# Loads of X^T, W and the Toeplitz tile issued at other places of a channel's order, each large load behind a compute instruction

## The chip, the cores and the metric

The kernel runs on one core of a Trainium2 chip. The metric is the device time of one execution in microseconds. Beside three timed executions there is one that the hardware profiler recorded; durations, waits and distances below come from that one. It has its own device time (878.34 us), and a span, from the program's first instruction to its last (876.5 us).

## The reference

For each of 64 channels (C) and a batch of 4, on images of 256 x 256 in float32:

```
k[c]  = outer product of two learned filters hx[:, c], hy[:, c]
y     = causal 2-D convolution of x with k       (written as an FFT of size 512)
x1    = y + x * bias[c]
scores = x1 @ x1^T / sqrt(256)                    (per image)
red   = sum over t of scores[s, t] * weights[c, s, t]
y2    = x1 + red
out   = (y2 - mean) * rsqrt(var + 1e-5) * gamma[c] + beta[c]
        (mean and var over batch, rows and columns of the channel)
```

Because the 2-D kernel is an outer product, the convolution is two 1-D convolutions, one along each axis. Each is a multiplication by a Toeplitz matrix.

## The kernel before

The 64 channels are worked one after the other, each in three groups of TensorE work, written by hand in an order that the kernel keeps (`manual_schedule`); the framework only adds the semaphores that the data needs, and allots buffers.

- `conv_z(c, m)`, m = 0, 1 (line 209): multiplies X^T by the Toeplitz rows along one axis, into PSUM. `copy_z` (218, ScalarE) copies each half out to the tile z.
- `conv_x0(c)` (234): multiplies z by the Toeplitz rows along the other axis. `add_bias` (244, VectorE) adds x * bias and writes x1.
- `gram(c, v)`, v = 0, 1 (297): x1 @ x1^T, in blocks. On VectorE `weigh` follows (317 and 321: product with W, pr and two partial sums) and `spread` (331). After both halves `all_sum` (339, GpSimd) sums over the partitions and gives red.

The rest of a channel comes later, in the iterations of the next channels. In iteration c, with p = c-1, q = c-2, f = c-3, e = c-4: `pick_red(p)` (346, ScalarE) waits for the sum over the partitions and copies half of red; `add_red(p)` (353, VectorE) adds red and sums; `minus_mean(q)` (388, 389) and `squares(q)` (393) are ScalarE's; `root(q)` (405 to 409) too; `finish` (433) scales a quarter of channel f or e on ScalarE, and its output transfer (434) is issued right behind it from SP.

All large transfers of the loop are issued by SP in one queue, in the order of the program. Per channel these are four outputs (256 KB each), four quarters of X^T by `load_xt` (256 KB each), W by `load_w` (320 KB), and the Toeplitz tile in four quarters by `load_h(c+2, 0..3)` (36 KB each, line 186). An output waits for ScalarE's finish. The Toeplitz tile has only its lower 64 partitions loaded; `copy_h` (191, ScalarE), the first ScalarE instruction of an iteration, copies them to the upper 64, and `conv_z` reads both halves: its second matmul reads the upper one. The tile of channel c+2, loaded in iteration c, is copied at the start of iteration c+1, and read by conv_z(c+2) in that iteration.

TensorE's order in iteration c is conv_x0(c), conv_z(c+1, 0), conv_z(c+1, 1), gram(c, 0), gram(c, 1). The loop runs to c = 61; `last_channels` has the rest in an order of its own, which the diff leaves as it is.

Of the kernel before, what the change touches and what calls it, by code (L numbers as in the profile page):

```python
# [9 lines left out]
AF = mybir.ActivationFunctionType  # L10
# [5 lines left out]
B, C, S = 4, 64, 256  # L16
# [21 lines left out]
def conv_scores_bn_kernel(  # L38
# [19 lines left out]
    nc = tc.nc  # L58
# [6 lines left out]

    xts, ws, hs = {}, {}, {}

    def load_xt(c, v, n):
        if not n:
            xts[c, v] = ld.tile([P, 4, S], F32, tag=f"xt{v}", name=f"xt_{c}_{v}", bufs=4)  # L70
        part = bass.ts(n, 2)
        nc.sync.dma_start(xts[c, v][:, part], xT[c, v, :, part])

    PARTS = ((0, 0), (1, 0), (0, 1), (1, 1))

    def load_w(c):
        w = ld.tile([P, 10, H], F32, tag="w", name=f"w_{c}", bufs=2)
        nc.sync.dma_start(w, wl[c])
        ws[c] = w


# [94 lines left out]
    def load_h(c, n):  # L176


        if not n:
            hs[c] = ld.tile([P, 2, GW], F32, tag="toep", name=f"toep_{c}")  # L180
        src = bass.AP(
            g_dram.tensor, g_dram.offset + c * 2 * GW + 16 * n,
            [[4 + C * 2 * GW, COPIES], [1, 4], [1, GW + S]],
        )
        rows = hs[c][bass.ts(n, 16)].rearrange("p a r -> p (a r)")
        nc.sync.dma_start(rows[:, : GW + S], src)

    def copy_h(c):

        toep = hs[c]  # L190
        nc.scalar.copy(toep[H:, :, :S], toep[:H, :, :S])  # L191
# [5 lines left out]
    st8, zs = {}, {}  # L197

    def conv_z(c, m):


        toep = hs[c]
        p1 = [ps.tile([P, 2, S], F32, tag="ps", name=f"p1_{c}_{m}_{u}") for u in range(2)]
        for k in range(2):
            for i in range(4):
                for t in range(4):
                    u, v = t % 2, t // 2
                    rows = bass.ts(u, H)
                    nc.tensor.matmul(  # L209
                        p1[u][bass.ts(v, H), k, : S - H * i],  # L210
                        lhsT=xts[c, v][rows, i, bass.ts(2 * m + k, H)],
                        rhs=toep[rows, 1, H * i : S], start=(i == 0), stop=(i == 3),
                    )
        return p1

    def copy_z(c, m, p1):
        for u in range(2):
            nc.scalar.copy(zs[c][:, u, bass.ts(m, 2), :], p1[u][:, :, ::-1])  # L218

    def conv_x0(c, z, parts=range(2)):  # L220

# [50 lines left out]
    def begin(c):  # L272
        x0 = wk.tile([P, 2, 4, S], F32, tag="x0", name=f"x0_{c}", bufs=5)
        red0 = sm.tile([P, B, 2], F32, tag="red0", name=f"red0_{c}")
        sp = wk.tile([P, B, S], F32, tag="sp", name=f"sp_{c}")
        pr = wk.tile([P, B, S], F32, tag="pr", name=f"pr_{c}")
        rd = wk.tile([P, B, S], F32, tag="rd", name=f"rd_{c}")
        st8[c] = (x0, red0, sp, pr, rd)
# [3 lines left out]
    def gram(c, v, weighed=True):  # L282


        xb = st8[c][0].rearrange("p v i (t s) -> p v i t s", s=H)
        gs = [ps.tile([P, 8, H], F32, tag="ps", name=f"g_{c}_{v}_{u}") for u in range(2)]

        for places in (
            ((0, slice(0, 3), slice(0, 5, 2)), (1, slice(1, 4), slice(2, 7, 2))),
            ((2, slice(2, 4), slice(3, 7, 3)), (3, slice(0, 4, 3), slice(0, 4, 3))),  # L290
        ):
            for i in range(4):
                for n in range(4):
                    u, h = n % 2, n // 2
                    rows = bass.ts(u, H)
                    m, t, o = places[h]
                    nc.tensor.matmul(  # L297
                        gs[u][bass.ts(h, H), o, :],
                        lhsT=xb[rows, v, i, m, :], rhs=xb[rows, v, i, t, :],
                        start=(i == 0), stop=(i == 3),  # L300
                    )
        if not weighed:
            banks.extend(gs)
            return
        for u in range(2):
            weigh(c, 2 * v + u, gs[u])
        if c < BY_PE:
            for u in range(2):
                spread(c, 2 * v + u)

    def weigh(c, b, g):

        _, red0, _, pr, _ = st8[c]
        w = ws[c]
        for n, part in enumerate((ROW0, ROW1)):
            junk = wk.tile([P, 3, H], F32, tag="junk", name=f"junk_{c}_{b}_{n}")
            nc.vector.scalar_tensor_tensor(  # L317
                junk, g[:, part, :], 1.0 / math.sqrt(S), w[:, 3 * n : 3 * n + 3, :],
                ALU.mult, ALU.mult, accum_out=red0[:, b, n : n + 1],
            )  # L320
        nc.vector.scalar_tensor_tensor(  # L321
            pr[:, b].rearrange("p (t s) -> p t s", s=H), g[:, COL, :], 1.0 / math.sqrt(S),
            w[:, 6:10, :], ALU.mult, ALU.mult,
        )

    def spread(c, b):

        _, red0, sp, pr, _ = st8[c]
        for n in range(2):
            part = bass.ts(n, P)  # L330
            nc.vector.scalar_tensor_tensor(  # L331
                sp[:, b, part], eye_sb, red0[:, b, n : n + 1], pr[:, b, part],
                ALU.mult, ALU.add,
            )
# [13 lines left out]
    def add_red(c):  # L348

        x0, _, _, _, rd = st8[c]  # L350
        mom = sm.tile([P, 8], F32, tag="mom", name=f"mom_{c}")
        for v in range(2):
            nc.vector.scalar_tensor_tensor(  # L353
                x0[:, v], x0[:, v], 1.0, rd[:, 2 * v, None, :].to_broadcast([P, 4, S]),
                ALU.mult, ALU.add, accum_out=mom[:, v : v + 1],
            )
        nc.gpsimd.partition_all_reduce(mom[:, 2:4], mom[:, 0:2], P, RED.add)  # L357
        return mom
# [27 lines left out]

    def minus_mean(mom):
        nc.scalar.activation(mom[:, 4:5], mom[:, 2:3], AF.Identity, bias=mom[:, 3:4])  # L388
        nc.scalar.activation(mom[:, 5:6], mom[:, 4:5], AF.Identity, scale=-1.0 / (B * S * S))

    def squares(c, mom, v):
        sq = wk.tile([P, 4, S], F32, tag="sq", name=f"sq_{c}_{v}", bufs=1)
        nc.scalar.activation(  # L393
            sq, st8[c][0][:, v], AF.Square, bias=mom[:, 5:6], accum_out=mom[:, 6 + v : 7 + v]
        )

    def sum_squares(c, mom):
        tot = sm.tile([P, 3], F32, tag="tot", name=f"tot_{c}")
        nc.gpsimd.partition_all_reduce(tot[:, 0:2], mom[:, 6:8], P, RED.add)  # L399
        return tot  # L400
# [25 lines left out]
    def finish(c, g, sh, v, n, vector=False):  # L426
        part = bass.ts(n, 2)
        o = wk.tile([P, 2, S], F32, tag="o", name=f"o_{c}_{v}_{n}", bufs=8)
        y = st8[c][0][:, v, part]
        if vector:  # L430
            nc.vector.tensor_scalar(o, y, g, sh, ALU.mult, ALU.add)
        else:
            nc.scalar.activation(o, y, AF.Identity, bias=sh, scale=g)  # L433
        nc.sync.dma_start(out[c, v, n], o)
# [130 lines left out]
    def begin_z(c):  # L565
        zs[c] = wk.tile([P, 2, 4, S], F32, tag="z", name=f"z_{c}")
# [6 lines left out]
    for c in range(C - 2):  # L573
        p, q, f, e = c - 1, c - 2, c - 3, c - 4
        begin(c)
        copy_h(c + 1)
        if e >= 0:
            finish(*fins[e], 0, 1)
        if c + 2 < C and c:
            load_xt(c + 2, 1, 1)  # L580
        load_h(c + 2, 0)
        conv_x0(c, zs.pop(c))
        if q >= 0:
            minus_mean(moms[q])
            squares(q, moms[q], 0)
        if e >= 0:
            finish(*fins[e], 1, 0)
        if c + 3 < C:
            load_xt(c + 3, 0, 0)
        load_h(c + 2, 1)  # L590
        if q >= 0:
            squares(q, moms[q], 1)
            tot = sum_squares(q, moms[q])
        if f >= 0:
            fins[f] = (f, *scale_shift(f, moms.pop(f), *scales.pop(f)))
        begin_z(c + 1)
        copy_z(c + 1, 0, conv_z(c + 1, 0))
        if e >= 0:
            finish(*fins.pop(e), 1, 1)
        load_h(c + 2, 2)  # L600
        if c + 3 < C:
            load_xt(c + 3, 1, 0)
        load_w(c + 1)
        load_h(c + 2, 3)
        copy_z(c + 1, 1, conv_z(c + 1, 1))
        if p >= 0:
            pick_red(p)
        if f >= 0:
            finish(*fins[f], 0, 0)
        if c + 3 < C:  # L610
            load_xt(c + 3, 0, 1)
        if q >= 0:
            scales[q] = root(q, tot)
        gram(c, 0)
        if p >= 0:
            moms[p] = add_red(p)
        gram(c, 1)
        if c < BY_PE:
            all_sum(c)
# [72 lines left out]
```

## Time and profile before

| | |
|---|---|
| median of 3 executions | 879.99 us (877.52 to 881.45) |
| profiled execution | 878.34 us, span 876.5 us |
| TensorE matmuls, weight loads | busy 98%, 96% of the span |
| VectorE, ScalarE, GpSimd | busy 86%, 71%, 49% |
| DMA queue of SP | 165.52 MB, 57.5% of 16 engines' time |
| output, X^T, W, Toeplitz transfers | 256, 256, 64 and 252 issues |

In rows of the timeline the first number is the start in us, the second the time taken; then the engine and the line of the kernel, the operation, what is written from what is read, and how many instructions were merged. SPq rows are the issue of a transfer, not its movement: when its data land stands in the records of the packets. In the waits view a row says which engine and line stood, for whom, how many us in total, how many times, and the longest. In square brackets stands the idle time before an instruction and what ended it. The start of a channel's conv_z is that of its first weight load of line 209.

### The profile page before, as it was taken

The numbers are of one execution on the slowest core, as the hardware profiler recorded it, in microseconds if no ns is written. First come the engines' busy times: TensorE is split into PE (matmuls) and PEld (weight loads), VectorE is DVE, ScalarE is ACT, GpSimd is POOL, SyncE is SP. The second block draws the span as 40 slices with busy tenths as digits, with TensorE's granted clock in tenths as the row PEclk, the third lists the DMA queues.
The fourth block names the chain that finished last, engine by engine and source line by source line (L and its number), as shares of the span: only waits on it lengthen the run. The fifth ranks groups of instructions, "written<-read, shape, count | busy, mean of one in ns | idle before, by whom it ended". The sixth has DMA issues, their size and how long they took to land.

```text
span 876.5 us, 55956 instructions
## 1 busy us (share of the span) xinstructions
PE 856.5 (98%) x24676; PEld 841.9 (96%) x24676; DVE 754.8 (86%) x2642; ACT 620.5 (71%) x1212; POOL 425.4 (49%) x195
## 2 busy tenths in 40 slices
PE   7999999999999999999999999999999999999993
PEld 5999999999999999999999999999999999999992
DVE  3588898898898898898898898898898898898886
ACT  2256777777776777777777776776777776776785
POOL 0236546545545545545645645645545545645600
PEclk9999999999999999999999999999999999999998
DMA  6624666666556565666566666666566666566534
GB/s 188 221 76 141 204 196 205 193 206 205 197 200 205 192 203 202 200 204 206 191 208 198 200 203 201 199 206 201 183 208 200 196 204 199 189 203 209 190 141 169
DMA packets 89870, 169.69 MB, mean 194 GB/s; under 512 B 10555, under 2 KB 11740, under 8 KB 89628
## 3 DMA queue, kind: packets, MB, share of 16 engines
q1 hardware_dynamic: 88972, 165.52, 57.5%
q8 instruction: 194, 3.18, 1.6%
q10 hardware_dynamic: 656, 0.59, 0.2%
q14 instruction: 48, 0.39, 0.2%
HBM read 98.18 MB, written 67.76 MB: 189 GB/s over the span
## 4 chain that ended last, share of the span: by engine, by line
PE 97%; DVE 1%; DMA 0%; ACT 0%; issue 0%; ACTq 0%; DVEq 0%
PE g L297 32%; PE p L209 32%; PE p L234 31%; PE p L263 0%; DMA fw_sb<-in_fw 0%; PE rp L368 0%; PE rp L373 0%; PE idle L166 0%; DVE x L382 0%; ACT o L433 0%; PE ph L146 0%; PE ph L130 0%; DVE fa L133 0%; DVE junk L317 0%; DVE fa L138 0%
## 5 line engine op out<-in xcount | busy, mean ns | idle before, releaser
L339 POOL PARTITION_ALL_REDUCE rd<-sp x61 | 373.5, 6124 | 182.3 <-DVE sp L331 182.3
L209 PE MATMUL p<-toep,xt 64*64 64x128 f32 (+3 forms) x8192 | 303.7, 297 | 0.6 <-issue 0.5
L297 PE MATMUL g<-x 64*64 64x192 f32 (+1 forms) x8192 | 302.1, 296 | 0.0
L234 PE MATMUL p<-toep,z 64*64 64x128 f32 (+3 forms) x8064 | 298.9, 296 | 0.0
L209 PEld LDWEIGHTS p<-toep,xt 64*64 64x64 f32 x8192 | 292.3, 133 | 5.7 <-PE idle L166 1.1
L234 PEld LDWEIGHTS p<-toep,z 64*64 64x64 f32 x8064 | 292.3, 133 | 4.1 <-issue 0.4
L297 PEld LDWEIGHTS g<-x 64*64 64x64 f32 x8192 | 288.6, 133 | 0.5 <-issue 0.2
L317 DVE SCALAR_TENSOR_TENSOR junk<-g,w 128x192 f32<-128x192 f32 x512 | 161.0, 352 | 83.0 <-PE g L297 83.0
L433 ACT ACTIVATE o<-x,sh,g 128x512 f32<-128x512 f32 x253 | 204.2, 811 | 3.1
L244 DVE SCALAR_TENSOR_TENSOR x<-xt,chan_sb,p 128x512 f32<-128x512 f32 x256 | 174.0, 741 | 8.4 <-PE p L263 7.3
L218 ACT COPY z<-p 128x512 f32<-128x512 f32 x256 | 134.7, 577 | 27.0 <-PE p L209 27.0
L393 ACT ACTIVATE sq<-x,mom 128x1024 f32<-128x1024 f32 x128 | 146.4, 1144 | 4.4 <-DVE x L382 2.0
L353 DVE SCALAR_TENSOR_TENSOR x<-x,rd 128x1024 f32<-128x1024 f32 x122 | 144.2, 1219 | 0.1
L331 DVE SCALAR_TENSOR_TENSOR sp<-eye_sb,red,pr 128x128 f32<-128x128 f32 x488 | 138.0, 345 | 0.0
L357 POOL PARTITION_ALL_REDUCE mom<-mom x61 | 24.4, 401 | 231.6 <-DVE x L353 227.5
L346 ACT COPY rd<-rd 64x512 f32<-64x512 f32 x61 | 37.6, 616 | 127.9 <-POOL rd L339 127.9
L321 DVE SCALAR_TENSOR_TENSOR pr<-g,w 128x256 f32<-128x256 f32 x256 | 107.4, 420 | 0.0
L191 ACT COPY toep<-toep 64x512 f32<-64x512 f32 x63 | 38.9, 618 | 42.8 <-DMA toep<-g_dram 32.6
L317 DVE DVE_READ_ACCUMULATOR junk<-g,w 128x1 f32 x512 | 42.5, 83 | 0.0
L388 ACT ACTIVATE mom<-mom 128x1 f32<-128x1 f32 x62 | 18.1, 292 | 32.0 <-POOL mom L357 31.8
L399 POOL PARTITION_ALL_REDUCE tot<-mom x62 | 29.8, 481 | 9.4 <-ACT sq L393 9.4
L393 ACT ACTIVATION_READ_ACCUMULATOR sq<-x,mom 128x1 f32 x128 | 23.8, 186 | 0.0
(62 smaller groups left out, 217.1 us busy)
## 6 DMA issues: line engine op xcount, KB each, us to landing
xt<-in_xT SPq DMA_DIRECT2D x256, 256.0 KB
out<-o SPq DMA_DIRECT2D x256, 256.0 KB
w<-in_wl SPq DMA_DIRECT2D x64, 320.0 KB
toep<-g_dram SPq DMA_DIRECT2D x252, 36.0 KB
g_dram<-g_sb SPq DMA_DIRECT2D x1, 320.0 KB
g_dram<-g_sb ACTq DMA_DIRECT2D x1, 320.0 KB
decay_sb<-in_decay SPq DMA_DIRECT2D x1, 256.0 KB
fw_sb<-in_fw ACTq DMA_DIRECT2D x1, 192.0 KB
```

Source lines behind the costliest of these rows:

```text
L209: nc.tensor.matmul(p1[u][bass.ts(v, H), k, : S - H * i], lhsT=xts[c, v][rows, i, bass.ts(2 * m + k, H)], rhs=toep[rows, 1, H * i : S], sta ...
L218: nc.scalar.copy(zs[c][:, u, bass.ts(m, 2), :], p1[u][:, :, ::-1])
L234: nc.tensor.matmul(p2[v][bass.ts(u, H), i, : S - H * k], lhsT=z[rows, u, k, bass.ts(2 * m + i, H)], rhs=toep[rows, 0, H * k : S], start=(k ...
L244: nc.vector.scalar_tensor_tensor(st8[c][0][:, v, part], xts[c, v][:, part], chan_sb[:, 0, c : c + 1], p2[v][:, :, ::-1], ALU.mult, ALU.add,)
L297: nc.tensor.matmul(gs[u][bass.ts(h, H), o, :], lhsT=xb[rows, v, i, m, :], rhs=xb[rows, v, i, t, :], start=(i == 0), stop=(i == 3),)
L317: nc.vector.scalar_tensor_tensor(junk, g[:, part, :], 1.0 / math.sqrt(S), w[:, 3 * n : 3 * n + 3, :], ALU.mult, ALU.mult, accum_out=red0[: ...
L321: nc.vector.scalar_tensor_tensor(pr[:, b].rearrange("p (t s) -> p t s", s=H), g[:, COL, :], 1.0 / math.sqrt(S), w[:, 6:10, :], ALU.mult, A ...
L331: nc.vector.scalar_tensor_tensor(sp[:, b, part], eye_sb, red0[:, b, n : n + 1], pr[:, b, part], ALU.mult, ALU.add,)
L339: nc.gpsimd.partition_all_reduce(rd.rearrange("p b s -> p (b s)"), sp.rearrange("p b s -> p (b s)"), P, RED.add)
L353: nc.vector.scalar_tensor_tensor(x0[:, v], x0[:, v], 1.0, rd[:, 2 * v, None, :].to_broadcast([P, 4, S]), ALU.mult, ALU.add, accum_out=mom[ ...
L393: nc.scalar.activation(sq, st8[c][0][:, v], AF.Square, bias=mom[:, 5:6], accum_out=mom[:, 6 + v : 7 + v])
L433: nc.scalar.activation(o, y, AF.Identity, bias=sh, scale=g)
```

## The change

Five transfers per channel get an extra semaphore wait on SP: a load is issued only after a certain instruction of ScalarE or VectorE has ended (`behind`, which adds a dependency on a marked instruction). The places in SP's order change with it. Before and after, for one iteration c of the loop:

```
before                         after
out finish(e,0,1)              out finish(e,0,1)
xt (c+2,1,1)                   toep(c+2) quarter 0
toep(c+2) quarter 0            xt (c+2,1,1)     after the mean of q (389)
out finish(e,1,0)              out finish(e,1,0)
xt (c+3,0,0)                   toep(c+2) quarter 1
toep(c+2) quarter 1            xt (c+3,0,0)     after copy_z(c+1, 0), u = 0
out finish(e,1,1)              out finish(e,1,1)
toep(c+2) quarter 2            toep(c+2) quarter 2
xt (c+3,1,0)                   w (c+1)          after copy_z(c+1, 1), u = 1
w (c+1)                        xt (c+3,1,0)     after pr of b = 0 (321)
toep(c+2) quarter 3            out finish(f,0,0)
out finish(f,0,0)              toep(c+2) quarter 3
xt (c+3,0,1)                   xt (c+3,0,1)     after add_red(p), v = 0 (353)
```

In the program gram(c, 0) now stands ahead of pick_red(p), finish(f, 0, 0) and root(q). The core of the diff:

```diff
+    marks = {}
+
+    def behind(load, place):
+        if place in marks:
+            tc.add_manual_dep(
+                load.ins, marks[place].ins.name,
+                mybir.DependencyInfo(mybir.DependencyClass.Sync, mybir.DependencyReason.DATA),
+                reason="pace of the loads",
+            )
...
-        nc.sync.dma_start(xts[c, v][:, part], xT[c, v, :, part])
+        load = nc.sync.dma_start(xts[c, v][:, part], xT[c, v, :, part])
+        behind(load, place)
...
-        nc.sync.dma_start(w, wl[c])
+        load = nc.sync.dma_start(w, wl[c])
+        behind(load, place)
...
         copy_h(c + 1)
         if e >= 0:
             finish(*fins[e], 0, 1)
-        if c + 2 < C and c:
-            load_xt(c + 2, 1, 1)
         load_h(c + 2, 0)
         conv_x0(c, zs.pop(c))
         if q >= 0:
             minus_mean(moms[q])
             squares(q, moms[q], 0)
+        if c + 2 < C and c:
+            load_xt(c + 2, 1, 1, "mean")
         if e >= 0:
             finish(*fins[e], 1, 0)
-        if c + 3 < C:
-            load_xt(c + 3, 0, 0)
         load_h(c + 2, 1)
...
         copy_z(c + 1, 0, conv_z(c + 1, 0))
+        if c + 3 < C:
+            load_xt(c + 3, 0, 0, ("z", 0, 0))
         if e >= 0:
             finish(*fins.pop(e), 1, 1)
         load_h(c + 2, 2)
+        copy_z(c + 1, 1, conv_z(c + 1, 1))
+        load_w(c + 1, ("z", 1, 1))
+        gram(c, 0)
         if c + 3 < C:
-            load_xt(c + 3, 1, 0)
-        load_w(c + 1)
-        load_h(c + 2, 3)
-        copy_z(c + 1, 1, conv_z(c + 1, 1))
+            load_xt(c + 3, 1, 0, ("pr", 0))
         if p >= 0:
             pick_red(p)
         if f >= 0:
             finish(*fins[f], 0, 0)
-        if c + 3 < C:
-            load_xt(c + 3, 0, 1)
+        load_h(c + 2, 3)
         if q >= 0:
             scales[q] = root(q, tot)
-        gram(c, 0)
         if p >= 0:
             moms[p] = add_red(p)
+        if c + 3 < C:
+            load_xt(c + 3, 0, 1, ("add", 0))
         gram(c, 1)
```

More of the change, by code (lines that the diff above doesn't have):

```diff
@@ L66, in conv_scores_bn_kernel, with load_xt @@
     xts, ws, hs = {}, {}, {}
-    def load_xt(c, v, n):
+    marks = {}
[6 more added lines that the diff above has]
+            )
+    def load_xt(c, v, n, place=None):
         if not n:
@@ L71, in load_xt, with load_w @@
         part = bass.ts(n, 2)
-        nc.sync.dma_start(xts[c, v][:, part], xT[c, v, :, part])
+        load = nc.sync.dma_start(xts[c, v][:, part], xT[c, v, :, part])
+        behind(load, place)
     PARTS = ((0, 0), (1, 0), (0, 1), (1, 1))
-    def load_w(c):
+    def load_w(c, place=None):
         w = ld.tile([P, 10, H], F32, tag="w", name=f"w_{c}", bufs=2)
-        nc.sync.dma_start(w, wl[c])
+        load = nc.sync.dma_start(w, wl[c])
+        behind(load, place)
         ws[c] = w
@@ L217, in copy_z @@
         for u in range(2):
-            nc.scalar.copy(zs[c][:, u, bass.ts(m, 2), :], p1[u][:, :, ::-1])
+            marks["z", m, u] = nc.scalar.copy(zs[c][:, u, bass.ts(m, 2), :], p1[u][:, :, ::-1])
     def conv_x0(c, z, parts=range(2)):
@@ L320, in weigh @@
             )
-        nc.vector.scalar_tensor_tensor(
+        marks["pr", b] = nc.vector.scalar_tensor_tensor(
             pr[:, b].rearrange("p (t s) -> p t s", s=H), g[:, COL, :], 1.0 / math.sqrt(S),
@@ L352, in add_red @@
         for v in range(2):
-            nc.vector.scalar_tensor_tensor(
+            marks["add", v] = nc.vector.scalar_tensor_tensor(
                 x0[:, v], x0[:, v], 1.0, rd[:, 2 * v, None, :].to_broadcast([P, 4, S]),
@@ L388, in minus_mean @@
         nc.scalar.activation(mom[:, 4:5], mom[:, 2:3], AF.Identity, bias=mom[:, 3:4])
-        nc.scalar.activation(mom[:, 5:6], mom[:, 4:5], AF.Identity, scale=-1.0 / (B * S * S))
+        marks["mean"] = nc.scalar.activation(
+            mom[:, 5:6], mom[:, 4:5], AF.Identity, scale=-1.0 / (B * S * S)
+        )
     def squares(c, mom, v):
```

## The prediction

> **What bounds the kernel now.** The page first: its busy line and the chain that ended last.
>
> ```profile
> span 876.5 us, 55956 instructions
> PE 856.5 (98%) x24676; PEld 841.9 (96%) x24676; DVE 754.8 (86%) x2642; ACT 620.5 (71%) x1212; POOL 425.4 (49%) x195
> PE 97%; DVE 1%; DMA 0%; ACT 0%; issue 0%; ACTq 0%; DVEq 0%
> ```
>
> TensorE is the whole chain. The chain in order of time shows its rhythm:
>
> ```profile
> 94.70 4.30 PE g L297 x118
> 107.78 4.30 PE g L297 x118
> 120.86 4.30 PE g L297 x118
> ```
>
> One channel takes 13.08 us. I took the start of each channel's conv_z from the weight loads of line 209: from the second channel to the last, 56 of 62 distances are within 0.01 us of 13.08, and the six others (13.19, 13.16, 13.48, 13.89, 13.14, 13.44) exceed it by 1.8 us together. So a change that moves transfers can win about 1.8 us in the loop; what stands before (15.74 us to the first conv_z) and after (837.25 to 876.5) has other code. The question is what it can lose: which work reaches TensorE with little to spare. The waits name one transfer:
>
> ```profile
> ACT rd L346 <- POOL rd L339: 127.9, 60, 2.4
> ACT toep L191 <- DMA toep<-g_dram: 32.6, 36, 2.5
> ```
>
> copy_h (line 191) waits for the last quarter of the Toeplitz tile in 36 of 63 channels, and TensorE's next conv_z reads the half that copy_h writes. The timeline of one channel (426 us) shows the cover:
>
> ```profile
> 422.20 0.34 SPq L434 DMA_DIRECT2D out<-o  x1
> 422.59 0.63 SPq L186 DMA_DIRECT2D toep<-g_dram  x1
> 423.32 0.39 SPq L72 DMA_DIRECT2D xt<-in_xT  x1
> 423.80 0.94 SPq L78 DMA_DIRECT2D w<-in_wl  x1
> 424.80 0.63 SPq L186 DMA_DIRECT2D toep<-g_dram  x1
> 425.42 0.61 ACT L346 COPY rd<-rd 64x512 f32<-64x512 f32 x1 [2.29 <-POOL rd L339]
> 426.06 0.81 ACT L433 ACTIVATE o<-x,sh,g 128x512 f32<-128x512 f32 x1
> 426.90 0.34 SPq L434 DMA_DIRECT2D out<-o  x1
> 427.29 0.93 SPq L72 DMA_DIRECT2D xt<-in_xT  x1
> 428.24 0.62 ACT L191 COPY toep<-toep 64x512 f32<-64x512 f32 x1 [0.67 <-DMA toep<-g_dram]
> 430.15 0.19 PEld L209 LDWEIGHTS p<-toep,xt 64*64 64x64 f32 x2
> ```
>
> The fourth quarter is issued at 424.80, copy_h ends at 428.86, conv_z starts at 430.15: 1.3 us to spare (median over the loop 1.5).
>
> **What the Trainium skill says.** "Perfetto Trace Analysis", section "DMA Instruction — HWDGE (DVE, Sync)": the sequencer waits for all semaphores of a DMA before issuing, so a wait on SP holds what is queued behind. The trace agrees: SP stands before every output until ScalarE is done (427.29 to 429.72 holds only one xt). "DMA: Bandwidth & Descriptors", section "Queues, rings and completion order": one queue's descriptors are taken in ring order, so a small load stands behind large ones ahead of it; the fourth quarter, behind xt and W, takes a median 3.00 us from issue to its last packet, the third, behind one output, 2.14. The same page, "Latency and other measured facts": some 2 us of a DMA are fixed; here no quarter was under 1.96.
>
> **The change, part by part.** (1) G's first half before the copy of red: gram issues only on TensorE and VectorE; pick_red, finish and root only on ScalarE and SP. Between conv_z's second half and add_red the order on TensorE, VectorE, ScalarE and POOL stays; cost 0. Its effect is that the product mark exists when xt is loaded. (2) Five waits on SP per channel: mean, two z copies, first product, first add of red. Unstalled these end 0.3, 3.9, 6.0, 8.0 and 11.1 us after conv_z's start (timeline of the channel at 403.99: 404.32, 407.93, 410.07, 412.04, 415.12). Each comes after the output ahead of it on SP and before the one behind it, so it holds no output. xt(c+2,1,1) is needed a channel later (11 us of cover); other xt have more, W 12 us; SP issue is 0.4 us each. Cost 0, unless that cover falls to 3 us.
> (3) **The fourth load_h moves** behind finish(f,0,0), hence behind W, xt and an output that waits for pick_red, which waits for POOL. That is not free. From the rows above:
> pick_red starts 425.42; finish ends 426.06+0.81 = 426.87; its output is issued 426.90 and the load 0.39 later, as 422.20 to 422.59: 427.29, i.e. 1.87 after pick_red and 2.49 later than now. Then issue to last packet: the nearest row is the third quarter, also right behind an output: median 2.14, mean of the loop 2.41, 1.96 to 3.86, by the packet records (16 packets of 2304 bytes each). Then 0.44 to the copy's start (mean of the 49 copies before which ScalarE stood over 0.1 us), 0.62 the copy. Sum with the median: 1.87+2.14+0.44+0.62 = 5.07 after pick_red. conv_z starts 4.73 after pick_red here (430.15-425.42), 4.88 in the first third, 4.93 in the last quarter. TensorE stands a little of it: at 286.19 a copy ended 0.30 after conv_z's start and that channel lost 0.08, so 0.22 is free. Lateness e with the median: +0.12 middle, -0.03 and -0.08 elsewhere; with each channel's own latency of the third quarter (60 channels) the mean of e is +0.30.
> A late conv_z moves the rest along: red's sum runs conv_z, gram, VectorE, POOL (6.12), pick_red, and its load serves the conv_z two channels on. So start(k+2) = the later of start(k+1)+13.08 and start(k)+26.16+e. Lower end: half the sum of all e, 8.9 us. Upper: each positive e paid in full, 19.7. The rule run over the 60 latencies in order: 13.8 us, which I take.
> Bounds of the unknown latency: at 1.96 throughout, e is -0.26 to -0.06 and the cost 0; W and xt, ahead of it in the queue (about 411.4 and 412.0 in the channel at 403.99, where it comes at 414.2), could leave a queue (now 576 KB of W and xt are through 3.5 us after the second's issue, so till about 415.5, while the output's packets, 1.4 us after its issue at 413.82, begin near 415.2), which adds up to 0.3 us: 22 us. (4) ScalarE follows copy_h 2.2 us later: from copy_h's end to the last z copy it works 7.1 us without waits (402.06 to 410.07 less 0.89), so that ends 7.4 after conv_z's start; conv_x0 asks for it at 8.7: 1.3 us of cover, cost 0.
>
> Sum against the profiled execution (878.34, of which 876.5 are the span): 878.3+13.8 = 892.1. The median of the runs shown, 879.99, lies 1.65 higher, within their spread of 3.9.
>
> **The rivals.** A (0.62): as above, copy_h late by some tenths in many channels, 884.4 to 905, likeliest 892. For it: the chain of rows; against it: a margin of 0.1 us decides.
> B (0.24), not slower: the Toeplitz load is still hidden. W and both xt are spread, so the fourth quarter could land as the third does in quiet channels (2.0 to 2.1), and copy_h end less than 0.22 us after conv_z's start; it decides at a latency of about 2.0 (middle) to 2.2 (last part). Price 0, perhaps some of the 1.8 us back: 877 to 884.
> C (0.08), faster: the six long channels and the spread of the runs (877.5 to 881.5) come from bursts of loads that meet instruction fetches. The Trainium skill, "Runtime: NRT & Kernel Launch", section "Instruction fetch mechanics", says that programs are refilled in 16 KiB blocks by DMA; the page agrees (194 packets, 3.18 MB). Without any stall the profiled execution would take 876.5, which against the median is 0.4%; more needs something that the profile doesn't show. 874 to 875.6.
> D (0.06), much slower: the late copy makes ScalarE the bound. It decides when copy_h ends over 1.4 us after conv_z's start, a latency of 3.4 us as behind W now; then z copies, too, stop TensorE; 1 us in half of the channels gives 30 us: over 905.
> That the waits don't take effect would show as A too, since the move of the load doesn't depend on them.
>
> **How the numbers follow.** About 0.5% (4.4 us) is what a measurement of this kernel can tell from no change: faster C 0.08, same B 0.24, slower A and D 0.68. The range from 877 to 905 takes A (own range 884.4 to 905) and nearly all of B, some 0.83.
>
> **What would show it.** Right: the wait of ScalarE's line 191 for the Toeplitz DMA grows from 33 us to over 100 in some 60 channels; the SP row of the fourth quarter stands 0.4 us after an output, 2.9 us before conv_z; distances of conv_z become 13.1 to 13.6, often alternating; TensorE shows idle before line 209 put down to ScalarE's toep. pick_red still waits for POOL. Wrong: copy_h ends before conv_z's start, distances stay 13.08 (B), or the z copies of line 218 come late and line 234 waits (D). What would make it wrong is above all the latency of that one load.

## The result, and the profile after

The changed kernel takes 907.86 us (median of 6 executions, 903.17 to 914.13), the kernel before 878.65 us in the same comparison (877.46 to 881.45). The ratio is 1.0337, with a 95% interval from 1.0315 to 1.0359: slower by 29 us. The forecast was 892 us, with a range up to 905. The direction and the place were right, the size was less than half.

The profiled execution of the changed kernel took 903.17 us, with a span of 901.4 us. It is the fastest of the six; what the slower ones have besides was not recorded. First the page: its span, its busy line, and the shares of the chain that ended last.

```profile
span 901.4 us, 56189 instructions
PE 876.9 (97%) x24676; PEld 843.0 (94%) x24676; DVE 755.0 (84%) x2642; ACT 615.0 (68%) x1212; POOL 425.4 (47%) x195
PE 88%; DVE 6%; DMA 3%; ACT 1%; issue 1%; POOL 1%; SPq 0%; ACTq 0%; DVEq 0%; POOLq 0%
```

The instructions of the busy line are the same in number as before, and VectorE, ScalarE and GpSimd are busy as long as before. PE is listed as busy 20 us longer for the same matmuls, so its busy time hides the stall; PEld's has grown by 1 us only. In the chain TensorE has gone from 97% to 88%, and VectorE, DMA and GpSimd have grown: the chain leaves TensorE, and goes back through a transfer to what this transfer waited for. The waits of the changed kernel say where (line 204 is copy_h, which was 191; 222 is conv_z, 209 before; 359 is pick_red, 346 before):

```profile
ACT toep L204 <- DMA toep<-g_dram: 129.2, 44, 4.8
ACT rd L359 <- POOL rd L352: 49.9, 52, 2.4
ACT toep L204 <- DMA xt<-in_xT: 36.4, 11, 4.2
PEld p L222 <- ACT toep L204: 11.0, 34, 0.5
```

copy_h stood 33 us for its Toeplitz tile before, and 129 us now. The row that names xt is the same wait: copy_h reads no X^T, and the releaser is inferred from semaphores that transfers of all kinds share. The last row did not exist before: TensorE waits for copy_h, inside conv_z. It shows 11 us only, because in part of the channels the first weight load of conv_z already comes late: over channels 2 to 62 it starts 9.5 us in all after conv_x0's last one, where it was 1.7 before.

The timeline of one channel of the changed kernel, from POOL's sum to conv_z. SPq rows are issues; the bracket is the idle time and what ended it. Only the rows that bear on the quarter are shown, here and in the timeline of e1 below.

```profile
105.64 6.12 POOL L352 PARTITION_ALL_REDUCE rd<-sp  x1 [2.43 <-DVE sp L344]
110.60 0.59 SPq L90 DMA_DIRECT2D w<-in_wl  x1
111.53 0.78 SPq L83 DMA_DIRECT2D xt<-in_xT  x1
111.80 0.62 ACT L359 COPY rd<-rd 64x512 f32<-64x512 f32 x1 [1.40 <-POOL rd L352]
112.44 0.81 ACT L448 ACTIVATE o<-x,sh,g 128x512 f32<-128x512 f32 x1
113.28 0.34 SPq L449 DMA_DIRECT2D out<-o  x1
113.68 0.63 SPq L199 DMA_DIRECT2D toep<-g_dram  x1
114.61 0.32 SPq L83 DMA_DIRECT2D xt<-in_xT  x1
116.96 0.62 ACT L204 COPY toep<-toep 64x512 f32<-64x512 f32 x1 [3.01 <-DMA xt<-in_xT]
117.63 1.50 PEld L222 LDWEIGHTS p<-toep,xt 64*64 64x64 f32 x42 [0.47 <-ACT toep L204]
```

The fourth quarter is issued at 113.68, 1.88 us after pick_red's start at 111.80; its last packet ends at 116.53 by the packet records, 2.86 us later; the copy runs from 116.96 to 117.58, and TensorE goes on at 117.63 after 0.47 us without a weight load.

From the weight loads of line 222 come the distances between the conv_z of successive channels: 9 of the last 62 are within 0.02 us of 13.08, the median is 13.39, the longest 14.43. What they have over 13.08 sums to 25.7 us; before it was 1.8. That is 23.9 of the 24.9 us by which the span grew. The first two conv_z come 0.4 us earlier, and from the last conv_z to the end it takes 40.6 instead of 39.3 us. So nearly all of the loss in this execution lies in the loop.

### The profile page after: what moved, and what is told of

The parts are those of the page before. It is cut to its first block, busy times and chain, and to the rows that moved or that the text cites. A ratio compares the mean times of both kernels' runs of the same rounds, so it can differ in the third digit from the quotient of the medians.

```text
span 901.4 us, 56189 instructions
## 1 busy us (share of the span) xinstructions
PE 876.9 (97%) x24676; PEld 843.0 (94%) x24676; DVE 755.0 (84%) x2642; ACT 615.0 (68%) x1212; POOL 425.4 (47%) x195
## 4 chain that ended last, share of the span: by engine, by line
PE 88%; DVE 6%; DMA 3%; ACT 1%; issue 1%; POOL 1%; SPq 0%; ACTq 0%; DVEq 0%; POOLq 0%
PE p L222 32%; PE g L310 28%; PE p L247 25%; DMA toep<-g_dram 2%; DVE junk L330 2%; DVE x L366 1%; DVE pr L334 1%; DMA xt<-in_xT 1%; DVE sp L344 1%; ACT o L448 1%; POOL rd L352 1%; PE p L276 0%; PE rp L381 0%; PE rp L386 0%; DMA toep<-g_sb 0%
## 5 line engine op out<-in xcount | busy, mean ns | idle before, releaser
L222 PE MATMUL p<-toep,xt 64*64 64x128 f32 (+3 forms) x8192 | 318.7, 298 | 5.1 <-DVE pr L334 1.3
L310 PE MATMUL g<-x 64*64 64x192 f32 (+1 forms) x8192 | 305.8, 296 | 0.0
L247 PE MATMUL p<-toep,z 64*64 64x256 f32 (+3 forms) x8064 | 302.8, 296 | 0.0
L408 ACT ACTIVATION_READ_ACCUMULATOR sq<-x,mom 128x1 f32 x128 | 23.9, 186 | 0.0
L431 DVE TENSOR_SCALAR u<-v,r 128x1 f32<-128x1 f32 x62 | 16.9, 273 | 6.7
```

Source lines behind the costliest of these rows:

```text
L222: nc.tensor.matmul(p1[u][bass.ts(v, H), k, : S - H * i], lhsT=xts[c, v][rows, i, bass.ts(2 * m + k, H)], rhs=toep[rows, 1, H * i : S], sta ...
L247: nc.tensor.matmul(p2[v][bass.ts(u, H), i, : S - H * k], lhsT=z[rows, u, k, bass.ts(2 * m + i, H)], rhs=toep[rows, 0, H * k : S], start=(k ...
L310: nc.tensor.matmul(gs[u][bass.ts(h, H), o, :], lhsT=xb[rows, v, i, m, :], rhs=xb[rows, v, i, t, :], start=(i == 0), stop=(i == 3),)
L408: nc.scalar.activation(sq, st8[c][0][:, v], AF.Square, bias=mom[:, 5:6], accum_out=mom[:, 6 + v : 7 + v])
```

## The experiments

Every ratio is to the kernel before, timed between the same executions on the same chip. The runs were taken in several sets, and the median of the kernel before went from 878.65 to 884.02 us between them, so kernels of different sets are compared by their ratios. In the tables, latency is the time from the issue of the fourth quarter (or what takes its place) to the end of its last packet, mean over channels 6 to 62. Excess is what the distances of conv_z have over 13.08. Both come from the one profiled execution of each kernel. The six executions of the changed kernel alone spread by 11 us, so a difference in latency is relied on below only where the ratios differ too.

**The quarter back in front of the output (e1).** Everything else of the change stays, the five waits too.

```diff
+        load_h(c + 2, 3)
         if p >= 0:
             pick_red(p)
         if f >= 0:
             finish(*fins[f], 0, 0)
-        load_h(c + 2, 3)
```

> The change, but the fourth quarter of the Toeplitz tile goes ahead of finish(f,0,0) again, behind W and the first xt (c+3,1,0); the five waits and the gram order stay. Theory T (the late quarter is the whole loss): it is issued about 4.5 us before conv_z instead of 3.3 to 3.9, lands 3.0 to 3.5 us later behind W and xt, copy_h ends 0 to 0.5 us before conv_z: 877 to 884 us. Rival W (the waits on SP themselves hold up transfers that are needed): still 895 to 910. Rival S (ScalarE has become the bound through the waits): 890 to 905.

882.43 us beside 883.2: ratio 1.000 (0.998 to 1.002). The loss is gone, as expected if the quarter is all of it. The timeline of this kernel shows the cover that has come back:

```profile
425.32 0.61 ACT L359 COPY rd<-rd 64x512 f32<-64x512 f32 x1 [1.61 <-POOL rd L352]
425.43 0.63 SPq L199 DMA_DIRECT2D toep<-g_dram  x1
426.81 0.34 SPq L449 DMA_DIRECT2D out<-o  x1
429.05 0.62 ACT L204 COPY toep<-toep 64x512 f32<-64x512 f32 x1 [1.57 <-DMA toep<-g_dram]
430.17 0.14 PEld L222 LDWEIGHTS p<-toep,xt 64*64 64x64 f32 x1
```

The quarter is issued 0.11 us after pick_red's start, not 1.88, and copy_h ends 0.5 us before conv_z. copy_h still waits, 62 us for toep by the waits view, and that costs nothing: it has the cover. The waits on SP cost nothing here either.

**The move alone (e2), and the gram alone (e4).** In the kernel before, only the one line is moved (e2), or only gram(c, 0) (e4).

```diff
-        load_h(c + 2, 3)
         copy_z(c + 1, 1, conv_z(c + 1, 1))
...
             finish(*fins[f], 0, 0)
+        load_h(c + 2, 3)
         if c + 3 < C:
             load_xt(c + 3, 0, 1)
```

> The kernel before, with only the fourth quarter moved behind finish(f,0,0) and its output; no waits, gram where it was. Theory T: most of the loss is here; issue 1.88 us after pick_red, latency 2.2 to 2.5 us because W and xt are out of the queue by then: 890 to 903 us (about +12 with the latencies that I took in the prediction, +19 with those measured in the changed kernel). Rival W: 876 to 883.

930.58 us, ratio 1.0535 (1.0478 to 1.0593). The place is confirmed, the size missed again: the move alone costs more than the whole change. The latency is 3.38 us, and the waits of this kernel show the same two rows, grown:

```profile
ACT toep L191 <- DMA toep<-g_dram: 158.4, 44, 4.8
PEld p L209 <- ACT toep L191: 15.3, 46, 0.5
```

> The kernel before, with only G's first half moved ahead of the copy of red. Both theories: no engine's own order changes, 877 to 881 us. If it differed by more than 4 us, the framework's semaphores would depend on the order of the program in a way that I have not seen.

882.73 us, ratio 0.9997 (0.9976 to 1.0017): the gram order costs nothing.

**The change without its waits (e3).** The five waits are dropped, the places kept.

```diff
-        if place in marks:
+        if False and place in marks:
```

> The change without its five waits; every transfer keeps its new place in SP's order. Theory T, with the waits as what lengthens the latency (W and xt then go out some tenths to 1 us earlier, and no longer stand ahead of the output and the quarter): latency of the quarter back from 2.64 to about 2.4 us in the mean, 889 to 900 us. If the waits don't matter to the latency: 903 to 910. Rival W: 876 to 884.

918.01 us, ratio 1.0398 (1.0353 to 1.0443); latency 3.09 us instead of 2.65. None of my three expectations held: without the waits it is not better but, if anything, worse (the interval overlaps with the change's, 1.0315 to 1.0359). e13 below shows that one of the waits does help once the quarter is late. What the other moved places are worth, between this kernel and e2, was not separated.

**How much each part of the quarter's way costs (e5, e6, e9).** In e5 the quarter stands ahead of the finish and waits for pick_red alone; in e6 it is issued behind ScalarE's finish but ahead of its output; in e9 it keeps its place, and W and xt(c+3,1,0) go behind it.

```diff
 # e5
+        load_h(c + 2, 3, "pick")      # marks["pick"] is pick_red's copy
         if f >= 0:
             finish(*fins[f], 0, 0)
-        load_h(c + 2, 3)
 # e6
-            finish(*fins[f], 0, 0)
-        load_h(c + 2, 3)
+            finish(*fins[f], 0, 0, ahead=lambda: load_h(c + 2, 3, "fin"))
...                                  # finish runs `ahead` between its activation (marks["fin"]) and its output
 # e9
-        load_w(c + 1, ("z", 1, 1))
         gram(c, 0)
-        if c + 3 < C:
-            load_xt(c + 3, 1, 0, ("pr", 0))
...
         load_h(c + 2, 3)
+        load_w(c + 1, ("z", 1, 1))
+        if c + 3 < C:
+            load_xt(c + 3, 1, 0, ("pr", 0))
```

> The change, with the fourth quarter ahead of finish(f,0,0), but made to wait for pick_red: issued 0.65 us after pick_red's start, 1.2 us earlier than in the change, and not behind that output. Theory T (its time of issue, plus its way through the queue, is the loss): 877 to 888 us; the rule of the prediction with the latencies measured in the changed kernel gives +2 us over no stall at all. If a wait for red's sum is ruinous by itself, however early: over 895.

> The change, with the fourth quarter issued behind ScalarE's finish(f,0,0), but ahead of its output on SP: 1.49 instead of 1.88 us after pick_red, and 256 KB fewer ahead of it in the queue. If only the time of issue counts (0.39 us): 895 to 900 us, the rule gives 8 us less than in the change. If the output ahead also holds it in the queue: latency down by 0.2 us or more, 884 to 894.

> The change, with W and xt (c+3,1,0) moved behind the fourth quarter, which keeps its time of issue 1.88 us after pick_red, behind the output. If W and xt ahead of it in the queue make its latency: the latency falls from 2.64 to about 2.15 us, and the cost of the change from 29 us to 0 to 8: 878 to 888 us. If the time of issue makes it: 900 to 910.

| kernel | issue after pick_red | latency | excess | median us | ratio (95%) |
|---|---|---|---|---|---|
| e1 | 0.21 | 2.85 | 3.2 | 882.43 | 1.000 (0.998 to 1.002) |
| e5 | 0.69 | 2.58 | 7.0 | 883.63 | 1.000 (0.998 to 1.002) |
| e6 | 1.49 | 2.32 | 5.0 | 884.34 | 1.002 (1.000 to 1.004) |
| e9 | 1.89 | 2.16 | 11.9 | 889.27 | 1.009 (1.006 to 1.011) |
| change | 1.95 | 2.65 | 25.7 | 907.86 | 1.034 (1.032 to 1.036) |

Up to 1.49 us after pick_red the stall is hidden; 0.4 us later, behind the output, it costs 3.4%. e6 came out as expected if the output ahead also holds the load in the queue, but it moves the issue and the output together, so it does not price them apart. e9 shows how much is the queue: the issue is as late as in the change, but with W and xt out of the way the latency is 2.16 us, the 2.14 that I took from the third quarter, and three quarters of the loss are gone. It came out 1.3 us over the time that I expected. The waits of the kernel e9:

```profile
ACT toep L204 <- DMA toep<-g_dram: 90.7, 40, 2.7
PEld p L222 <- ACT toep L204: 2.4, 9, 0.4
```

copy_h still waits long, but TensorE waits for it 9 times, not 34.

**Why the latency is what it is (e8, e10, e13, e14, e15).** e8 gives ScalarE about 0.8 us per channel back (an activation of 1.14 us falls to some 0.3): the second half of the squares is taken over 8 of 256 columns. The variance then lacks most of that half, so e8, e14 and e15 serve for the timing alone. e10 drops the waits of W and of xt(c+3,1,0) alone, e13 that of xt(c+3,0,1) alone, which stands right behind the quarter. e14 is e13 with ScalarE relieved as in e8, e15 is e2 relieved.

```diff
 # e8, e14, e15
+        n = 8 if v else S
         nc.scalar.activation(
-            sq, st8[c][0][:, v], AF.Square, bias=mom[:, 5:6], accum_out=mom[:, 6 + v : 7 + v]
+            sq[:, :, :n], st8[c][0][:, v, :, :n], AF.Square, bias=mom[:, 5:6], accum_out=mom[:, 6 + v : 7 + v]
 # e10
-        load_w(c + 1, ("z", 1, 1))
+        load_w(c + 1)
...
-            load_xt(c + 3, 1, 0, ("pr", 0))
+            load_xt(c + 3, 1, 0)
 # e13, e14
-            load_xt(c + 3, 0, 1, ("add", 0))
+            load_xt(c + 3, 0, 1)
```

> The change, with the second half of the squares taken over 8 of 256 columns of each row (the variance then lacks most of that half), which gives ScalarE about 1.0 us per channel back between copy_h and the z copies. Theory T without ScalarE (the copy's lateness alone): unchanged, 903 to 910 us, since pick_red mostly waits for POOL (rule: 0.2 us less). Rival S (a late copy_h makes ScalarE late, which holds the outputs, and W and xt behind them, on SP, so that they stand close ahead of the quarter): latency of the quarter down to about 2.4 us in the mean, 885 to 897.

> The change without the waits of W and of xt (c+3,1,0), the two loads ahead of the late quarter; the other three waits stay. Without all five the quarter's latency was 3.09 us and the time 918. If these two waits are what keeps the queue short for the quarter: latency about 3.0 us, 912 to 920. If they are not: latency 2.5 to 2.7, 900 to 910, or less, since both loads then go out a little earlier.

> The change without the wait of xt (c+3,0,1), which stands right behind the late quarter and then goes out at once, some 0.9 us earlier. If a large load right behind the quarter slows it: latency about 3.0 us, 912 to 920. If only what stands ahead of it counts: latency 2.65 us, 903 to 910.

> The change without the wait of the load right behind the late quarter (as in e13), and with the second half of the squares over 8 of 256 columns (as in e8; the variance lacks most of that half). Feedback through ScalarE: the latency of the quarter is e8's, 2.3 to 2.45 us, and the time e8's, 893 to 902. The load right behind slows the quarter directly: latency 2.65 us or more, 904 to 915.

> The kernel before with only the fourth quarter moved (as in e2), and the second half of the squares over 8 of 256 columns. Feedback: latency falls from 3.38 to about 2.5 us, 893 to 905. Direct: latency stays over 3.0, 915 to 930.

| kernel | latency | excess | median us | ratio (95%) |
|---|---|---|---|---|
| e8: change, ScalarE relieved | 2.36 | 19.2 | 898.39 | 1.019 (1.013 to 1.024) |
| e10: change, waits of W and xt(c+3,1,0) off | 2.81 | 35.6 | 910.69 | 1.032 (1.029 to 1.035) |
| e13: change, wait of xt(c+3,0,1) off | 3.09 | 39.1 | 921.44 | 1.047 (1.042 to 1.052) |
| e14: e13, ScalarE relieved | 2.81 | 32.1 | 910.37 | 1.032 (1.025 to 1.040) |
| e3: change, all five waits off | 3.09 | 38.6 | 918.01 | 1.040 (1.035 to 1.044) |
| e2: quarter alone moved | 3.38 | 48.8 | 930.58 | 1.054 (1.048 to 1.059) |
| e15: e2, ScalarE relieved | 3.04 | 37.4 | 911.96 | 1.029 (1.022 to 1.037) |

Two things move the latency.

*Feedback through ScalarE*: relief takes 0.28 to 0.34 us off it in all three pairs (2.65 to 2.36, 3.09 to 2.81, 3.38 to 3.04) and 1.5 to 2.4 points off the ratio. A late copy_h delays ScalarE, which delays finish(e,1,1); on SP, W and xt stand behind that output, and so come closer to the quarter: W goes out 3.5 us ahead of it in e8, 2.6 in the change. Lateness alone does this too, with ScalarE's work as it was: in e1, e5, e6 and the change W has the same place in the order and the same wait, while the quarter is issued later from one to the next, and W goes out 1.7, 1.6, 1.1 and 0.5 us ahead of pick_red (means). Its own wait does not time it: in e10, without it, W goes out 2.6 us ahead of the quarter as before, and the ratio is that of the change, though in time e10 fell between my two expectations.

*The load right behind it*: without the wait of xt(c+3,0,1) the latency rises by about 0.44 us, with ScalarE relieved (2.36 to 2.81) as without (2.65 to 3.09), and the ratio by some 1.4 points in both pairs (1.034 to 1.047, 1.019 to 1.032), so this is not the feedback alone. W stands 0.2 to 0.3 us closer there as well; if 0.9 us closer is worth 0.29 us, as from e8 to the change, that is under 0.1 us of it (an estimate). e14 came out where the direct account had put it; e15 has its latency, but a time under it; e8 and e13 each ended 1.4 us above the time of the account that they support. The 0.3 us that the relief takes off belong to the feedback. So both act.

How a load that is issued after the quarter slows it is open. Its packets do not only overlap with the quarter's: the first packet of the quarter, too, starts 0.2 us later after its issue (1.81 instead of 1.60), though only 0.1 us later with ScalarE relieved (1.62 instead of 1.54). And in e9 W stands right behind the quarter, at 0.7 us, without harm, where one output is all that is large and close ahead.

The waits of e8 against those of the change show the relief:

```profile
ACT rd L359 <- POOL rd L352: 107.4, 60, 2.4
PEld p L222 <- ACT toep L204: 3.2, 11, 0.5
```

pick_red now stands 107 us for POOL, where it stood 50 in the change and 128 before. That wait is ScalarE's reserve, and the late copy_h had used up more than half of it.

**A version that beats both?** The fourth quarter right behind the third, in the change (e11) and in the kernel before (e12).

```diff
         load_h(c + 2, 2)
+        load_h(c + 2, 3)
...
-        load_h(c + 2, 3)
```

> The change with the fourth quarter right behind the third, ahead of W, both xt and the output: issued some 6 us before conv_z, latency about 2.3 us, so copy_h never late. Theory T: no stall before conv_z, 876 to 882 us where before has 880 to 883; it can win at most the 2 to 7 us that before loses in single channels. Rival W: slower than before by some us.

> The kernel before with the fourth quarter right behind the third, ahead of xt (c+3,1,0) and W; nothing else. Issued some 6.5 us before conv_z instead of 5.7, latency 2.3 instead of 3.1, so 1.5 us more to spare; copy_h late in no channel. 876 to 883 us: the same as before, or up to 3 us less if some of its long channels come from a late copy.

882.21 us, ratio 1.0009 (0.9990 to 1.0028), and 882.79 us, 1.0007 (0.9991 to 1.0023), beside 881.66. In both, copy_h ends 2.0 us before conv_z in the median, and neither gains: the single long channels are still there (excess 8.4 and 5.3 us in the profiled executions), so they don't come from this load. No version that I ran is faster than the kernel before.

## Why the prediction was right and wrong

**What bounds it, and what can be won.** Right. TensorE's 13.08 us per channel are a floor in every kernel here; spread loads win nothing (e1, e11). Rival C is refuted as far as these runs reach.

**Part 1, gram, at nothing.** Right: e4, 0.9997.

**Part 2, the waits, at nothing.** Right as a cost: with all five in, e1 stands at 1.000. What I did not see is that one of them is worth something once the quarter is late: without that of xt(c+3,0,1), the change goes from 1.034 to 1.047.

**Part 3, the moved quarter.** The mechanism and its place are shown: undoing that one line takes the loss away (e1), and making it alone brings more than the loss (e2). The issue 1.88 us after pick_red came as derived, in most channels to 0.01 us. The rule that a late conv_z pays half of e per channel is supported: over the nine kernels in which the quarter is issued 1.9 us after pick_red, the excess rises with the latency by 29 us per us (least squares over the values in the tables, deviations up to 3.9 us); half of the 57 channels in the mean is 28.5. Run in order over the changed kernel's own copies, with conv_z's time after pick_red as the prediction has it, the rule gives 22.6 of the 25.7 us; every lateness paid in full would be 40.5. The 3 us left are not assigned.

**The step that failed** is the latency of the moved load, "the nearest row is the third quarter, also right behind an output: median 2.14, mean of the loop 2.41". It measured 2.65 in the mean. That row has another neighbourhood: before, W and xt went out behind the third quarter, not ahead of it, and ScalarE was not late. The other terms were a little short too: 0.52 instead of 0.44 us from the last packet to the copy, and 1.95 instead of 1.87 to the issue, since the output's own issue is sometimes slow. The half rule gives 0.24 x 28.5 = 6.8 us, 2.3 and 2.3 us for the three, 11.4 together. With the 13.8 forecast that is 25.2; the loop grew by 23.9 in the profiled execution; that these agree so closely is in part chance, with 3 us not assigned above. I had named the queue of W and xt as worth up to 0.3 us, 22 us in all, and then taken zero: with that term the forecast would have been some 900 us (an estimate, 878.3 and 22). e9 shows what this queue is worth, with the feedback that works through it: 0.49 us.

**Part 4, ScalarE at nothing.** Wrong, and one reason why the latency was short. I gave the 7.1 us of ScalarE's work after copy_h a cover of 1.3 us towards conv_x0, and that held: the z copies stop nobody. But the work has a second deadline, pick_red. From copy_h's end to the earliest pick_red ScalarE takes 7.0 us in the changed kernel, nearly the same in every channel. pick_red stood 2.1 us per channel for POOL before, 0.8 after, and nothing at all in a few channels. Before pick_red's turn comes the output finish(e,1,1), with W and xt behind it on SP. So a ScalarE that holds up nobody on TensorE still sets when the loads go out; 0.8 us less of its work is worth 1.5 points of the ratio (e8).

**The range.** Its upper end, 905, was A's upper end; it held the profiled execution (903.17) but not the median. The rest between these two, 4.7 us, is the spread of the changed kernel's executions, 11 us against 4 before.

**The marks.** As listed: the wait for the Toeplitz tile above 100 us (though under this name in 44 channels, not 60; 11 more stand under xt's), the quarter 0.4 us behind an output (but 3.4 us before conv_z, not 2.9, since conv_z itself is late), TensorE idle for ScalarE's toep, pick_red still waiting for POOL (52 channels). The distances were 13.1 to 14.4, not to 13.6, and without a regular alternation. B fails by them; D does not apply, as the waits of the changed kernel have no row of conv_x0 for z. The prediction read copy_h's waits before as 36 of 63 channels from one row of the view; its own mean over 49 copies is the fuller count, as other rows name the same wait differently.

The Trainium skill's page "DMA: Bandwidth & Descriptors", section "Queues, rings and completion order", says that descriptors of a queue are taken in ring order on each engine; e9 agrees, with 0.49 us less for the quarter once 576 KB are out of its way. The prediction had cited this, and then not charged it. e13 shows that the order of the descriptors is not all: a load behind counts too.

## What to carry to other kernels

A small load that an engine at its bound needs next is priced by what stands around it in its queue at its new place, and not by a row from another neighbourhood; put it ahead of anything that waits for a late result. When a step is made late, list every deadline of the engine that it delays, the transfers issued behind that engine's results among them: they move closer to the late load, and make it later. A wait for which there is cover costs nothing, however long it is in the table (e1); the step from e6 to the change, 0.4 us and one output, cost 3% here, since nearly every channel pays it.

## What the runs showed of the hardware

A 36 KB load of 16 rows of 2304 bytes took 2.2 us from issue to its last packet with one output issued 0.4 us ahead of it and nothing else large in the 3.5 us before, though W 0.7 us behind (e9), and 3.4 us with an output, an xt, W and another output issued in the 3.3 us before it and an xt 0.7 us behind (e2). From the last packet to the start of the instruction that waited for it went about another 0.5 us (0.45 to 0.55 in the means of all kernels above but e11 and e12, where the copy waits for other work). With a 256 KB load issued 0.7 us after such a small one, instead of 1.2 to 1.3, the small one's latency was about 0.44 us higher (e13 against the change, e14 against e8, means of one execution each). I had not expected that of a queue taken in order, and can't explain it.
